# A graph layer's gathers: 71 single rows per half step in place of 40, fetched by two other queues

## Chip, cores and metric

The kernel runs on one core of a Trainium2 chip. The metric is device time in microseconds for one execution; the kernel before takes 15340.11 us in the median of three runs (15320.92 to 15340.7). The profiled execution is a fourth one.

## What is computed

There are 50,000 nodes with 128 features each and 1,650,000 edges, sorted by destination. 50,000 of the edges are self-loops, one for each node. The reference, cut down:

```
Xs  = x[src]
msg = where(edge_type == 0, Xs @ W_data.T + b_data, Xs @ W_control.T + b_control)
agg = segment_sum(msg, dst)
h   = relu(agg + x @ W_self.T + b_self)
out = layernorm(x + h)
```

For each edge a row of 512 bytes is fetched from `x`, and the rows are summed by destination and type. The kernel sums the raw rows first (two sums per node, one for each type) and multiplies the sums by the weights afterwards.

## The kernel before

The program is unrolled over NBLK = 510 steps. Each step but the first and the last takes BE = 3236 edges, in Q = 2 half steps of 1618. The edges of a half step are served in three ways:

- **1536 by gathers**: 12 columns of 128 edges. For each column GpSimd issues one indirect DMA (L477, `gathers`) that fetches 128 rows of `x` into a tile `y`. A tile holds PASS = 6 columns, and there are SLOTS = 10 such tiles, so GpSimd may run up to 60 gathers ahead of TensorE. That is 24 gathers for a whole step.
- **F = 42 fillers**: in the 1536 places some edges are self-loops, whose row need not be gathered because the step's own nodes are loaded in any case (`xT`, L406). `fill` (L316 to L338, VectorE) puts 42 other edges into 42 such places of the half step and notes which self-loops it pushed out. These are added from `xT` later (L345 to L370, L525).
- **S = 40 single rows**: plain DMAs of 512 bytes, each with its address in a register. TURNS = (20, 20) says how many of a half step's rows SP's queue and ScalarE's queue (ACT) issue. For the step, that is 40 copies on each.

`single_rows(b, part)` issues the single rows. A row of byte offsets, `at_x`, is written for the step by VectorE (L435). Each of the LOADS = 2 parts loads its share of the offsets into registers of the queue's engine with one load instruction (TENSOR_LOAD, L446, here 20 registers), and then issues a register move and a DMA for each row (L451). SP and ACT work side by side, each through its own half of `at_x`. When all rows of a step have landed, TensorE uses them in one product for each half step (L502), after the twelve gathered columns (L496).

**Order.** The schedule is written out by hand in the last loop of `straight`, and every engine follows its instructions in that order. Within step b the loop over four passes of six gathers places, among others:

- pass 0: six columns of products, then `layer(b-1)` (TensorE, L531 to L535), `moments(b-1)`, `onehot(b+2)`, and `single_rows(b+2, 0)`;
- pass 1: six columns, the first half's single rows (`rows_fetched` is TensorE's wait for them), `add(b, 0)` (L512), `root(b-1)` (ACT, L551), `counts(b+2)` (L420), `single_rows(b+2, 1)`;
- pass 2: six columns, `store(b-1)` (VectorE, L557 to L559), `fill(b+5)`;
- pass 3: six columns and the second half's single rows, `offsets(b+3)` (L435), `store_rows(b-1)` (SP, L563). The next step begins with `window(b+4)` (SP, L406) and `add(b, 1)`.

So on SP's queue, in each step: the parts of `single_rows(b+2)`, the store of the finished rows of step b-1 (which waits for VectorE's L559), the load of `xT` (with a load of five base registers in every fifth step, L400), and in every tenth step the loads of the edge lists of the next ten steps (L165 to L174) and the two transfers at L301 and L306. On ACT's queue: part 0 of `single_rows(b+2)`, the square root of step b-1, then the other part. The single rows of step b are therefore issued during step b-2, as soon as VectorE has written their offsets in step b-3's last pass. Four sets of `yx`, the tile that the rows land in, rotate (ROW_SLOTS).

The last step takes what is left: 3040 edges, all by gathers (24 of them). With the first step's 24 that makes 510 x 24 = 12,240 gathers. Ahead of the loop, VectorE prepares steps 1 to 4, and the single rows of step 1 are issued there.

Of the kernel before, what the change touches and what calls it, by code (L numbers as in the profile page):

```python
# [36 lines left out]
Q = 2  # L37
PASS = 6
B = 112
C = R * Q  # L40
F = 42
TURNS = (20, 20)
S = sum(TURNS)
LOADS = 2
X = Q * S
R1 = R + 1
C1 = Q * R1
SIZES = [P] * R
SIZE = sum(SIZES)
CE = Q * SIZE  # L50
BE = CE + Q * F + X
NBLK = 2 + (E - CE) // BE
REST = E - CE - (NBLK - 2) * BE
REST_ROWS = [min(n, max(0, REST - q * SIZE - sum(SIZES[:r]))) for q in range(Q) for r, n in enumerate(SIZES)]
# [23 lines left out]
TBL = GROUPS * GB  # L78
# [3 lines left out]
def plain(b):  # L82

    return b == 0 or b >= NBLK - 1
# [6 lines left out]
def straight(ctx, tc, c, x, x_t, src_t, dst_t, etype_t, src_f, dst_f, etype_f, src_x, dst_first, first_p, out):  # L91
# [35 lines left out]
                   allow_small_or_imprecise_dtypes=True)  # L127
    FILL = Q * F + C1
    small = keep_ps.tile([P, 2 * W + F + 2 * FILL + 2], F32, name="small")
    num_ps, rank_no_ps = small[:, :2 * W], small[:, 2 * W:2 * W + F]  # L130
    lists = [small[:, 2 * W + F + i * FILL:][:, :FILL] for i in range(2)]
    sums_at = [small[:Q * F, 2 * W + F + 2 * FILL + i:][:, :1] for i in range(2)]

# [29 lines left out]
    def load_edges(g):  # L163
        t = eds.tile([1, GB * X], I32, name="one_g")
        nc.sync.dma_start(t, src_x[None, g * GB * X:(g + 1) * GB * X])  # L165
        one_g[g] = t
        loads[g] = {}
        for name, a in (("s", src_t), ("d", dst_t), ("t", etype_t)):
            t = eds.tile([P, GB, C1], I32, name=name, bufs=1)
            nc.sync.dma_start(t.rearrange("p b c -> p (b c)"), a[:, g * GC:(g + 1) * GC])  # L170
            loads[g][name] = t
        for name, a in (("sf", src_f), ("df", dst_f), ("tf", etype_f)):
            t = eds.tile([GS, F], I32, name=name, bufs=1)
            nc.sync.dma_start(t, a[g * GS:(g + 1) * GS, :])  # L174
            loads[g][name] = t
# [54 lines left out]
    def check(d, rel, at, name):  # L230
        chk = eds.tile(list(d.shape), F32, name="chk" + name, bufs=1)
        nc.vector.scalar_tensor_tensor(chk, d, float(DST_PAD), rel, op0=ALU.is_lt, op1=ALU.mult)
        axes = AX.XY if len(d.shape) == 3 else AX.X
        nc.vector.tensor_reduce(at[0], chk, axes, ALU.min)
# [74 lines left out]
    def fill(b):  # L309
# [15 lines left out]
        v = fil.tile([P, C1], F32, name="v_new")  # L325
        nc.vector.tensor_reduce(v, new, AX.X, ALU.add)  # L326
        vi = fil.tile([P, C1], I32, name="vi")
# [9 lines left out]
        with nc.allow_low_precision(reason="whole numbers below 256, one of them not 0"):  # L337
            nc.vector.tensor_reduce(by, old.rearrange("p (q r) f -> p q f r", r=R1), AX.X, ALU.add)  # L338
        bys[b] = by
# [76 lines left out]
    def counts(b):  # L416

        cnt = ohp.tile([P, Q, 2 * W], BF16, name="cnt")
        with nc.allow_low_precision(reason="whole numbers up to R1"):
            nc.vector.tensor_reduce(cnt, ohs[b].rearrange("p (q r) w -> p q w r", r=R1), AX.X, ALU.add)  # L420
        cnts[b] = cnt
# [8 lines left out]
    def offsets(b):  # L430

        if not plain(b):
            g, i = divmod(b, GB)
            ats[b] = stp.tile([1, X], I32, name="at_x", bufs=AHEAD + 2)
            nc.vector.tensor_scalar(ats[b], one_g[g][:, i * X:(i + 1) * X], float(ROW), None, op0=ALU.mult)  # L435

    def single_rows(b, part):

        if part == 0:
            ys[b] = stp.tile([S, Q, D], F32, name="yx", bufs=ROW_SLOTS)  # L440
        both = []
        for j, (eng, dma) in enumerate(((SP, nc.sync), (ACT, nc.scalar))):
            n = Q * TURNS[j]
            k0, k1 = part * n // LOADS, (part + 1) * n // LOADS
            at = Q * sum(TURNS[:j])
            _, rows = nc.values_load_multi_w_load_instructions(ats[b][0:1, at + k0:at + k1], engines=[eng], **RANGE)  # L446
            both.append([(dma, fetched[j][b % ROW_SLOTS], *divmod(k0 + k, TURNS[j]), sum(TURNS[:j]), row)
                         for k, row in enumerate(rows)])
        for pair in zip_longest(*both):
            for dma, sem, q, k, at, row in filter(None, pair):  # L450
                copy = dma.dma_start(ys[b][at + k:at + k + 1, q, :].bitcast(U8), x_bytes[:, bass.ds(row, ROW)])  # L451
                copy.then_inc(sem, 16)
                tc.no_tile_sem_insts.add(copy.ins.name)
                tc.add_to_no_dep_group(f"single{b}", copy.ins)

    def rows_fetched(b):

        times = len(range(b % ROW_SLOTS or ROW_SLOTS, b + 1, ROW_SLOTS))
        for j in range(2):
            wait = nc.tensor.wait_ge(fetched[j][b % ROW_SLOTS], 16 * Q * TURNS[j] * times)  # L460
        tc.declare_fence(wait.ins, group=f"single{b}")
# [141 lines left out]
    for b in range(1, RAHEAD):  # L603
        fill(b)
        left_out_columns(b)
        left_out_matrix(b)
        if b < AHEAD:
            onehot(b)
            counts(b)
            for part in range(LOADS):  # L610
                single_rows(b, part)
        if b == 1:
            clear_sums()
    for b in range(NBLK + 1):
# [16 lines left out]
        for q, (step, ks) in enumerate(passes_of(b)):  # L631
# [26 lines left out]
            if q == 3:  # L658
                left_out_matrix(b + RAHEAD)
                offsets(b + AHEAD + 1)  # L660
            if q < LOADS and not plain(b + AHEAD):
                single_rows(b + AHEAD, q)
# [226 lines left out]
def gnn_resnorm(  # L889
# [50 lines left out]
    with ExitStack() as own:  # L940
        straight(own, tc, c, x, x_t, src_t, dst_t, etype_t, src_f, dst_f, etype_f, src_x,
                 dst_first, first_p, out)
# [58 lines left out]
```

## Time and profile before

| | |
|---|---|
| median of three runs | 15340.11 us (15320.92 to 15340.7) |
| profiled execution | 15323.45 us |
| its span, first to last instruction | 15321.7 us |
| granted TensorE clock, mean | 0.535 |
| GpSimd busy (DMA_INDIRECT) | 11565.0 us, 75% |
| VectorE busy | 10904.6 us, 71% |
| TensorE busy, matmul / weight load | 8296.6 us, 54% / 7096.5 us, 46% |
| ScalarE busy | 153.6 us, 1% |
| q0 (GpSimd's gathers) | 802.93 MB, 20.9% of the 16 DMA engines' time |
| q1 (SP) / q10 (ACT) | 112.76 MB, 2.9% / 10.68 MB, 0.3% |

An engine's busy time counts only its working instructions. Register, branch, semaphore and DMA-issuing instructions do not count as busy, so SP does not appear in the table, and ACT's 1% leaves out all its copies. Both are seen only in the timeline of their queues (SPq, ACTq) and in the list of the instructions of one line. In the timeline a row is a merged run of like instructions: its start, its length from the first one's start to the last one's end, and how many there were.

### The profile page before, as it was taken

What the parts mean: (1) busy time and instruction counts of PE and PEld (TensorE: products, weight loads), DVE (VectorE), ACT (ScalarE), POOL (GpSimd) and SP (SyncE); (2) the same over time, 40 slices, a digit from 0 to 9 for tenths busy, and PEclk for the clock granted to TensorE, in tenths of its full rate; (3) what the DMA queues carried; (4) which work ended last, traced back from release to release, by engine and by line L of the source; (5) the groups of instructions that cost most, each with busy time, mean ns of one, the idle gap of its engine ahead of it and who ended that gap; (6) DMA issues with size and microseconds to landing.
All of it is one profiled execution on the core that took longest, in us unless ns stands there. A gap on an engine that the chain in (4) does not pass through costs nothing. (4 is left out here: it accounts for less than half of the span.)

```text
span 15321.7 us, 197234 instructions
## 1 busy us (share of the span) xinstructions
PE 8296.6 (54%) x35844; PEld 7096.5 (46%) x35845; DVE 10904.6 (71%) x13994; ACT 153.6 (1%) x516; POOL 11565.0 (75%) x12250
## 2 busy tenths in 40 slices
PE   3555555555555555555555555555555555555555
PEld 3444444444444444444444444444444444444444
DVE  8777777777777777777777777777777777777775
ACT  0000000000000000000000000000000000000000
POOL 7777777777777777777777777777777777777777
PEclk7555555555555555555555555555555555555555
DMA  2222222222222222222222222222222222222222
GB/s 65 62 61 62 61 62 61 62 62 61 62 61 62 61 62 61 62 61 62 62 60 62 61 62 61 62 62 61 61 62 62 61 62 61 62 61 62 62 61 56
DMA packets 649293, 939.07 MB, mean 61 GB/s; under 512 B 327756, under 2 KB 445487, under 8 KB 648034
## 3 DMA queue, kind: packets, MB, share of 16 engines
q0 software_dynamic: 391680, 802.93, 20.9%
q1 hardware_dynamic: 215276, 112.76, 2.9%
q10 hardware_dynamic: 41078, 10.68, 0.3%
q14 instruction: 968, 7.93, 0.2%
q8 instruction: 291, 4.77, 0.1%
HBM read 895.92 MB, written 29.42 MB: 60 GB/s over the span
## 5 line engine op out<-in xcount | busy, mean ns | idle before, releaser
L477 POOL DMA_INDIRECT y<-in_x,idx x12216 | 11540.9, 945 | 3733.3 <-issue 3552.2
L496 PE MATMUL acc<-oh,y 128*128 128x120 f32 x24480 | 5867.6, 429 | 5768.3 <-PEq L484 5767.8
L496 PEld LDWEIGHTS acc<-oh,y 128*128 128x128 f32 x24480 | 5313.7, 326 | 6190.7 <-PEq L484 6178.3
L420 DVE TENSOR_REDUCE cnt<-oh 128x240 bf16<-128x3120 f32 x510 | 2959.6, 5803 | 0.1
L541 DVE COPY h<-po 112x128 f32<-112x128 f32 x510 | 148.7, 292 | 2499.1 <-PE po L535 2407.5
L412 DVE TENSOR_TENSOR oh<-col,small 128x3120 f32<-128x3120 f32 x510 | 1719.5, 3372 | 0.0
L512 DVE TENSOR_TENSOR sums<-acc,sums 128x180 f32 x1020 | 352.2, 345 | 1393.1 <-PE acc L505 1236.0
L338 DVE TENSOR_REDUCE by<-old 128x84 bf16<-128x1092 f32 x508 | 1078.5, 2123 | 17.6
L502 PE MATMUL acc<-oh,yx 40*128 40x120 f32 x2032 | 777.4, 484 | 0.0
L345 PE MATMUL small<-ones_b,by 128*84 128x1 bf16 x508 | 117.4, 231 | 1191.1 <-DVE by L338 1191.1
L319 DVE TENSOR_TENSOR m<-rk,small 128x1092 f32<-128x1092 f32 x508 | 656.4, 1292 | 17.3
L322 DVE TENSOR_TENSOR new<-m,small 128x1092 f32<-128x1092 f32 x508 | 656.2, 1292 | 17.3
L326 DVE TENSOR_REDUCE v_new<-new 128x26 f32<-128x1092 f32 x508 | 655.8, 1291 | 17.3
L345 PEld LDWEIGHTS <-by 128*84 128x84 bf16 x508 | 74.3, 146 | 1267.3 <-DVE by L338 1267.2
L335 DVE TENSOR_TENSOR old<-m,small 128x1092 f32<-128x1092 f32 x508 | 652.3, 1284 | 0.0
L502 PEld LDWEIGHTS acc<-oh,yx 40*128 40x128 f32 x2032 | 497.5, 304 | 210.0 <-issue 205.3
L535 PE MATMUL po<-wmsgT,sums 128*112 128x128 f32 x2040 | 515.1, 396 | 0.0
L535 PEld LDWEIGHTS po<-wmsgT,sums 128*112 128x112 f32 x2040 | 374.0, 253 | 108.2 <-issue 88.7
L533 PE MATMUL po<-bias,sums 3*112 3x128 f32 x1020 | 350.3, 439 | 0.0
L525 DVE TENSOR_TENSOR sums<-pl,sums 128x336 f32<-128x336 f32 x508 | 257.9, 508 | 85.2 <-DVE sums L512 84.6
L532 PE MATMUL po<-wselfT,xT 128*112 128x128 f32 x1020 | 315.5, 412 | 0.0
L551 ACT ACTIVATE sd<-mv,eps 112x1 f32<-112x1 f32 x510 | 150.4, 295 | 15051.3 <-DVE mv L546 8335.5
(118 smaller groups left out, 4174.2 us busy)
## 6 DMA issues: line engine op xcount, KB each, us to landing
yx<-in_x ACTq DMA_DIRECT2D x20320, 0.5 KB
yx<-in_x SPq DMA_DIRECT2D x20320, 0.5 KB
y<-in_x,idx POOLq DMA_INDIRECT x12216
xT<-in_x_t SPq DMA_DIRECT2D x510, 56.0 KB
out<-o SPq DMA_DIRECT2D x510, 56.0 KB
vf_all<-vd SPq DMA_DIRECT2D x51, 420.0 KB
s<-in_src_t SPq DMA_DIRECT2D x51, 130.0 KB
d<-in_dst_t SPq DMA_DIRECT2D x51, 130.0 KB
```

The costliest lines, as they stand in the source:

```text
L319: nc.vector.tensor_tensor(m, rk_g[g][:, i, :, None].to_broadcast([P, C1, F]), rank_no_ps[:, None, :].to_broadcast([P, C1, F]), op=ALU.is_e ...
L322: nc.vector.tensor_tensor(new.rearrange("p (q r) f -> p q r f", r=R1), m.rearrange("p (q r) f -> p q r f", r=R1), vf.rearrange("p (q f) -> ...
L326: nc.vector.tensor_reduce(v, new, AX.X, ALU.add)
L335: nc.vector.tensor_tensor(old, m, cb[:, :, None].to_broadcast([P, C1, F]), op=ALU.mult)
L338: nc.vector.tensor_reduce(by, old.rearrange("p (q r) f -> p q f r", r=R1), AX.X, ALU.add)
L412: nc.vector.tensor_tensor(oh, col_g[g][:, i, :, None].to_broadcast([P, C1, 2 * W]), num_ps[:, None, :].to_broadcast([P, C1, 2 * W]), op=AL ...
L420: nc.vector.tensor_reduce(cnt, ohs[b].rearrange("p (q r) w -> p q w r", r=R1), AX.X, ALU.add)
L477: copy = nc.gpsimd.indirect_dma_start(out=y[:r, k % PASS, :].bitcast(U8), out_offset=None, in_=x_rows, in_offset=bass.IndirectOffsetOnAxis ...
L496: nc.tensor.matmul(acc[:, :2, :].rearrange("p t w -> p (t w)"), y[:r, k % PASS, :], ohs[b][:r, column(k), :], start=k == of_step[0], stop= ...
L502: nc.tensor.matmul(acc[:, :2, :].rearrange("p t w -> p (t w)"), ys[b][:, q, :], ohs[b][:S, q * R1 + R, :], start=False, stop=True)
L512: nc.vector.tensor_tensor(part, accs.pop((b, q)), part, op=ALU.add)
L535: nc.tensor.matmul(po, a[:, t, :B], c["wmsgT"][:, t * D:(t + 1) * D], start=False, stop=t == 1)
```

## The change

Three constants, the split of a half step's single rows into parts, and the layout of the offsets:

```diff
-F = 42
-TURNS = (20, 20)
+F = 43
+TURNS = (35, 36)
 S = sum(TURNS)
-LOADS = 2
-X = Q * S
+LOADS = 3
+BEGIN = (0, -(-Q * TURNS[0] // 4) * 4)
+X = BEGIN[1] + -(-Q * TURNS[1] // 4) * 4
...
-BE = CE + Q * F + X
+BE = CE + Q * (F + S)
...
+    def part_of(n, part):
+
+        return n if part == LOADS else -(-part * n // (4 * LOADS)) * 4
+
...
-            k0, k1 = part * n // LOADS, (part + 1) * n // LOADS
-            at = Q * sum(TURNS[:j])
+            k0, k1 = part_of(n, part), part_of(n, part + 1)
+            at = BEGIN[j]
```

S becomes 71, and a step takes 3072 + 2 x (43 + 71) = 3300 edges. For a whole step SP issues 70 copies and ACT 72. Each queue's rows come in three parts (passes 0, 1 and 2) of 24, 24 and 22 registers on SP and 24, 24 and 24 on ACT. The parts begin at offsets 0, 24 and 48 of `at_x` for SP and at 72, 96 and 120 for ACT; `at_x` has 144 entries in place of 80. The rest of the diff lays the host's list of offsets out in the same way. There are 2 + (1650000 - 3072) // 3300 = 501 steps, and 228 edges are left for the last one, which are two gathers (128 and 100 rows).

## Prediction

> **What bounds the kernel now.** I read the costliest groups first, then the waits, then the timeline of GpSimd's queue in mid-run.
>
> ```profile
> L477 POOL DMA_INDIRECT y<-in_x,idx x12216 | 11540.9, 945 | 3733.3 <-issue 3552.2
> ...
> L420 DVE TENSOR_REDUCE cnt<-oh 128x240 bf16<-128x3120 f32 x510 | 2959.6, 5803 | 0.1
> ```
>
> GpSimd does little else than issue gathers: 945 ns busy each, and the idle time between them is nearly all "issue", in which it waits for nothing that the profile shows.
>
> ```profile
> 7004.21 0.94 POOL L477 DMA_INDIRECT y<-in_x,idx  x1 [0.30 <-issue]
> 7005.45 0.95 POOL L477 DMA_INDIRECT y<-in_x,idx  x1 [0.30 <-issue]
> 7006.71 0.94 POOL L477 DMA_INDIRECT y<-in_x,idx  x1 [0.30 <-issue]
> ```
>
> So a gather starts every 1.25 us, busy engine or not. The first starts at 3.2 us and the last at 15305.3 (the line's own list): 15302.1 / 12239 = 1.2503 us. 24 of them make a step of 30.0 us. Since 12,240 x 1.25 is the whole span, **the kernel's time is the number of gathers times 1.25 us**, plus 16.4 us after the last one's start. VectorE works 10904.6 / 510 = 21.4 us of those 30, TensorE's matmuls 16.3. They wait.
>
> The two queues that issue the single rows wait too. For SP the waits, the list of the load's and the copies' lines, and its timeline:
>
> ```profile
> SPq L446 <- DVE sums L525: 4574.7, 482, 41.1
> ```
>
> ```profile
> L446 ACTq TENSOR_LOAD <-at_x x1016: 1411/1437/1689, 16.8 to 15202.4; - x170
> L446 SPq TENSOR_LOAD <-at_x x1016: 1197/1378/1676, 26.8 to 15191.8; - x170
> ```
>
> ```profile
> L451 SPq MOVE yx<-in_x x20320: 29/29/37, 28.0 to 15199.5; - x200
> L451 SPq DMA_DIRECT2D yx<-in_x x20320: 224/228/389, 28.1 to 15199.6; - x200
> ```
>
> ```profile
> 7014.69 14.42 SPq L451 DMA_DIRECT2D yx<-in_x  x40
> 7029.38 0.34 SPq L563 DMA_DIRECT2D out<-o  x1
> 7029.90 0.36 SPq L406 DMA_DIRECT2D xT<-in_x_t  x1
> 7030.36 0.36 SPq L306 DMA_DIRECT2D vf_all<-vd  x1
> 7039.36 14.90 SPq L451 DMA_DIRECT2D yx<-in_x  x40
> ```
>
> The reader is to see that a burst of 40 copies takes SP some 14.7 us and that it then idles for 7 to 9 us until the next step's offsets are written. The change fills this room. The question is whether it overfills it.
>
> **The gathers that go.** 501 steps make 500 x 24 + 2 = 12,002 gathers, 238 fewer. At 1.25 us (no stall among those removed) that is 297.5 us. At the end a little comes back: the last step has 2 gathers in place of 24, so the end of the step before it no longer lies beside them. After its last gather follow the landing (2.4 us in the chain of before), 12 products, `find_bad`, two `add`s, and two layers with their moments one after the other. By the rows of the last 20 us of before I count 21.4 us from the last gather's start in place of 16.4, so +5. With GpSimd as the bound: 15321.7 - 297.5 + 5 = **15029 us of span**.
>
> **SP's step, before.** From the timeline between 7005 and 7310 us, ten bursts: 14.42, 14.90, 14.90, 14.47, 14.84, 14.83, 14.85, 14.46, 14.82, 14.85, mean 14.73 us, each with one load of 20 registers inside. Ahead of it lies the first load (1.36 us on the idle queue) with 0.12 us of gaps: 1.48. Other work of the step: store and `xT` 1.15 (7029.11 to 7030.26), a base load of 1.17 every fifth step (0.24), the ten-step group's nine DMAs (0.39). Sum 1.78. In all 1.48 + 14.73 + 1.78 = **17.99 us** of 30.
>
> **SP's step, after:**
> - 30 more copies. In a burst, a load amid it costs 1.58 us (1.46 right behind copies, gaps 0.06, a slower first copy 0.06). So a copy takes (14.73 - 0.23 - 1.58) / 39 = 0.33 us. Added: 9.90. Bounds: 0.322 from the shortest burst, 0.334 from the longest.
> - A third load: 1.58.
> - More registers in a load: 24, 24 and 22 for 20. The trace has no such load. One register takes SP 0.473 us (L943), five take 0.75 where they begin at a multiple of four and 1.30 where they don't (L400: 714/1286/1386), 20 take 1.36. This fits a price of 0.22 us for each group of up to four: (1.36 - 0.473) / 4. I take this, since it alone explains the two prices of L400: one more group in each of three loads is 0.66. Below it, by registers alone, (1.36 - 0.473) / 19 x 10 = 0.47. Above, 3 x 0.25 = 0.74, from 1.46 behind copies.
>
> Sum: 17.99 + 9.90 + 1.58 + 0.66 = **30.1 us**, with the low prices 29.7, with the high ones for every copy and load 30.6. Against GpSimd's 30.0 this is a tie, and it leans to SP.
>
> The page "Runtime: NRT & Kernel Launch" of the Trainium skill (Instruction fetch mechanics) speaks against the change: a register load costs about 200 ns for each register, even in bulk. This trace agrees only for L400's five registers that don't begin at a multiple of four (1.30 us); 20 in 1.38 to 1.44 us are 70 ns each. By the page, SP's 70 registers would cost 14 us and the step would be some 39 us, 19,600 us in all as an estimate.
>
> **ACT's step.** By the same count over its records it works 16.7 us of 30 now. 32 more copies at 0.327 (10.45), a third load with its slower first copy (1.77) and three more groups of registers (0.74) make 29.6. It stays under both, so it is hidden. Without SP's limit it would be next.
>
> **What the span is if SP is the bound.** SP can't hide its lag for long, for the start already uses the reserve. VectorE writes the offsets of step 3 only at 103.3 us, since it fills four steps first. Before, SP then has its rows issued in 16 us and the engines catch up about 5 us per step (their own work is 25 us). After, steps 3 to 499 follow without a pause: 497 steps x 30.1 from 103.5. Behind the last row come its landing and the products that it held back (some 10 us) and the end as above (19), less 1.8 of SP's work that comes later: + 27. So the span is 130 + 497p for a step of p us, and GpSimd's bound of 15029 takes over at p = 29.98. For p = 30.1: 130 + 14965 = **15095 us**. The profiled run's time was 1.75 us over its span: **15097**. That execution was 17 us under the median of the runs shown, within their scatter.
>
> **What costs nothing.** F = 43 lengthens five VectorE operations of a step by 1/42 (1.29 x 4 + 2.12, so 0.17 us) and the offsets by 64 numbers (below 0.1): hidden, as VectorE has 8 us to spare. A longer contraction in L502 (71 rows for 40) is the same instruction. Rows land late only if SP is late, which is counted. The gather's pitch doesn't suffer: among intervals with four SP copies in them it is 1.249 us, as in those with none. ACT's square root comes behind 24 copies in place of 20 (1.6 us later), and VectorE needs it only after 5.8 us of `counts`; without that cover `store` would stall 1.6 us per step, within the 8. The fillers need 43 self-loops in each half step; in the given edges the fewest is 43, so it just suffices and the general path isn't taken.
>
> **Rivals.**
> - **A: SP fits.** The offsets' loads cost by registers, or the copies run at their clear-run pitch of 0.3215 us (the median) when the queues no longer start in step with each other. Then p is under 29.98 and GpSimd keeps the bound: 15031 us. For it: the shortest bursts. Against: one copy in 67 has a gap of 0.33 us more, which grows with the number of copies.
> - **C: the copies slow down (slower).** Both queues now issue without a break. In the trace the second to sixth copies of a burst, where ACT starts beside SP, have a mean pitch of 0.331 to 0.346. Were all at 0.346, p = 30.1 + 70 x 0.016 = 31.2 and the time 130 + 497 x 31.2 = 15640. It decides from 0.338 (p = 30.66, 15370 us). Against: whole bursts stay at 0.334 or less.
> - **D: 24 registers don't fit one load**, so the change gives more loads than three. Three more (0.47 + 0.06 each) give p = 31.7: 15885 us. For it: no load in the trace has more than 20.
>
> **How the numbers follow.** B, the forecast (SP bound by a little, p from 29.98 to 30.66): 0.57; A 0.33; C 0.07; D 0.03. Differences under 0.2% are about what a measurement of this kernel can't tell from none; that band, 15309 to 15371, is the top of B (p over 30.53), 0.04. So faster 0.86, same 0.04, slower 0.10. The range goes from just under A's time, 15015, to p = 30.42, which is 15250: it leaves out C, D, and the top of B.
>
> **What would show it.** Gathers: 12,002 at 0.944 us. If B holds, SP's queue has no wait for offsets left, bursts of 70 stand 30.1 us apart, and GpSimd waits for TensorE's products (its tiles come free late), while TensorE waits for the single rows. If A, GpSimd's idle stays all "issue" and SP still idles a little. In both, loads of 24 registers take 1.58 to 1.7 us and copies 0.32 to 0.334. A load over 1.9 us or a pitch over 0.338 makes the prediction wrong.

## The result and the profile after

The changed kernel takes **15829.25 us** (median of four runs, 15826.12 to 15832.71), the kernel before 15340.1: a ratio of 1.0321 (95% interval 1.0305 to 1.0337). It is 3.2% slower, where 1.6% faster was forecast (15097). The profiled run took 15827.65 us, its span 15826.0.

GpSimd did lose its 238 gathers, and a gather takes as long as before. But now it stands still between them. Of the profile after, the costliest groups and the waits (engine, line, whom it waited for: us in total, times, longest):

```profile
L482 POOL DMA_INDIRECT y<-in_x,idx x12000 | 11339.4, 945 | 4422.8 <-issue 3422.7
```

```profile
PE acc L507 <- PEq L465: 3218.0, 392, 21.3
...
POOL y L482 <- PE acc L501: 792.8, 187, 11.1
```

GpSimd waits 793 us for a tile that TensorE hasn't used yet (L501). TensorE in turn stands at L507, the product of the single rows, behind L465: its wait until all rows of the step have landed. The list of that line's instructions shows how long one such wait lasts (minimum / median / maximum in ns). The first row is from the kernel before, where the line is L460, the second from after:

```profile
L460 PEldq EVENT_SEMAPHORE  x508: 51/51/51, 106.9 to 15263.1; - x170
```

```profile
L465 PEldq EVENT_SEMAPHORE  x499: 51/10226/23226, 108.1 to 15790.9; - x167
```

Before, the rows were always there. After, this wait lasts 10 us in the median step, and TensorE itself is idle for 3218 / 499 = 6.4 us of each step because of it. So the single rows set the pace. Who is late with them? SP's waits and its timeline:

```profile
SPq L175 <- DMA out<-o: 534.4, 49, 12.9
SPq L451 <- DVE mv L551: 40.9, 41, 1.8
```

```profile
7026.04 0.35 SPq L568 DMA_DIRECT2D out<-o  x1
7026.63 1.58 SPq L407 DMA_DIRECT2D xT<-in_x_t  x1
...
7030.63 0.34 SPq L175 DMA_DIRECT2D df<-in_dst_f  x1
7041.17 0.28 SPq L175 DMA_DIRECT2D tf<-in_edge_type_f  x1
7043.34 26.71 SPq L456 DMA_DIRECT2D yx<-in_x  x70
7070.31 0.35 SPq L568 DMA_DIRECT2D out<-o  x1
7070.89 0.36 SPq L407 DMA_DIRECT2D xT<-in_x_t  x1
7073.03 26.81 SPq L456 DMA_DIRECT2D yx<-in_x  x70
```

SP hardly waits for offsets any more (L451: the largest row is 41 us; L446 had 4575 us before). It works 30.5 us of each step, by the sum of its records and the short gaps between them. Yet a step takes 31.6 us, and the rest is one wait that wasn't there before: in every tenth step the last of the edge lists (`tf`, L175) stands 10 us. Its instruction uses the same completion semaphore as the store of rows (`out`) issued eight DMAs earlier at 7026.04, and waits until that has landed. The rows land as late; the chain that ended last holds such landings (start, length):

```profile
7025.50 15.02 DMA yx<-in_x
7069.82 11.56 DMA yx<-in_x
7221.04 8.27 DMA yx<-in_x
```

A copy of 512 bytes takes up to 15 us from its issue to its landing. From the trace's semaphore events I took, for each step between 1,000 and 14,000 us, the time from the last issue to the last landing of SP's rows: before 2.8 to 4.0 us, after 3.1 to 15.1. It grows by about 1.5 us from step to step for seven steps, from 4 us to 14 or 15, and falls back over the next three: SP stands at L175 for 10 us, and ACT then stands 15 us before a load of offsets. **The copies pile up behind the queues.**

The same events show where. A load of `xT` tells of its landing in sixteen events, and the profile counts 16 DMA engines. Medians from the start of its issue, for the loads with all sixteen events in the trace:

| | 15 of the 16 have come | all 16 |
|---|---|---|
| before | 1.90 us | 1.97 us |
| after | 1.96 us | 10.1 us |
| ACT's rows left out (an experiment below) | 1.89 us | 1.94 us |

Fifteen shares of `xT` land as early as before, and one lands as late as the rows. The store of `out` shows the same (1.65 and 10.1 us after the change), which is why it keeps L175 waiting. So the backlog lies in one place out of sixteen, and whatever has a share there waits with the copies.

### The profile page after: what moved, and what is told of

Its sections match the earlier page's. It is cut to its first block, busy times and chain, and to the rows that moved or that the text cites. A ratio compares the mean times of both kernels' runs of the same rounds, so it can differ in the third digit from the quotient of the medians.

```text
span 15826.0 us, 256554 instructions
## 1 busy us (share of the span) xinstructions
PE 6610.8 (42%) x35177; PEld 6147.3 (39%) x35178; DVE 10848.4 (69%) x13768; ACT 150.8 (1%) x507; POOL 11342.8 (72%) x12012
## 4 chain that ended last, share of the span: by engine, by line
SPq 35%; DVE 23%; DMA 15%; issue 14%; PE 8%; ACTq 4%; DVEq 0%; ACT 0%; PEldq 0%; PEld 0%
SPq L456 27%; DMA yx<-in_x 14%; SPq L451 7%; DVE cnt L421 5%; PE acc L501 4%; ACTq L456 4%; DVE by L339 3%; DVE m L320 2%; DVE new L323 2%; DVE v_new L327 2%; DVE old L336 2%; PE po L540 1%; PE acc L507 1%; DMA out<-o 1%; PE po L538 1%
## 5 line engine op out<-in xcount | busy, mean ns | idle before, releaser
L482 POOL DMA_INDIRECT y<-in_x,idx x12000 | 11339.4, 945 | 4422.8 <-issue 3422.7
L501 PE MATMUL acc<-oh,y 128*128 128x120 f32 x24004 | 4836.7, 384 | 0.1
L501 PEld LDWEIGHTS acc<-oh,y 128*128 128x128 f32 x24004 | 4598.7, 293 | 0.2 <-PE po L593 0.2
L507 PE MATMUL acc<-oh,yx 71*128 71x120 f32 x1996 | 560.2, 373 | 3218.4 <-PEq L465 3218.0
L507 PEld LDWEIGHTS acc<-oh,yx 71*128 71x128 f32 x1996 | 405.7, 253 | 3316.6 <-PEq L465 3316.0
L339 DVE TENSOR_REDUCE by<-old 128x86 bf16<-128x1118 f32 x499 | 1080.4, 2165 | 17.3
L320 DVE TENSOR_TENSOR m<-rk,small 128x1118 f32<-128x1118 f32 x499 | 658.6, 1320 | 17.0
L323 DVE TENSOR_TENSOR new<-m,small 128x1118 f32<-128x1118 f32 x499 | 658.5, 1320 | 17.1
L327 DVE TENSOR_REDUCE v_new<-new 128x26 f32<-128x1118 f32 x499 | 657.4, 1317 | 17.0
L336 DVE TENSOR_TENSOR old<-m,small 128x1118 f32<-128x1118 f32 x499 | 654.2, 1311 | 0.0
```

Of the source, the lines that this page charges most:

```text
L320: nc.vector.tensor_tensor(m, rk_g[g][:, i, :, None].to_broadcast([P, C1, F]), rank_no_ps[:, None, :].to_broadcast([P, C1, F]), op=ALU.is_e ...
L323: nc.vector.tensor_tensor(new.rearrange("p (q r) f -> p q r f", r=R1), m.rearrange("p (q r) f -> p q r f", r=R1), vf.rearrange("p (q f) -> ...
L482: copy = nc.gpsimd.indirect_dma_start(out=y[:r, k % PASS, :].bitcast(U8), out_offset=None, in_=x_rows, in_offset=bass.IndirectOffsetOnAxis ...
L501: nc.tensor.matmul(acc[:, :2, :].rearrange("p t w -> p (t w)"), y[:r, k % PASS, :], ohs[b][:r, column(k), :], start=k == of_step[0], stop= ...
L507: nc.tensor.matmul(acc[:, :2, :].rearrange("p t w -> p (t w)"), ys[b][:, q, :], ohs[b][:S, q * R1 + R, :], start=False, stop=True)
```

## The theories

- *Landing*: the copies of both queues pass one place that takes some 0.22 us for each. SP and ACT hand over 142 in the 30.5 us that SP works for a step, the place needs about 31.6, and the backlog grows until something waits for a landing.
- *Issue* (the forecast, with more in it): SP's instructions are the bound, 30.5 us, and the wait at L175 is an accident of the order, worth 1.1 us per step.

A step's length is given below as the mean distance of SP's stores, over whole tens of steps between 1,000 and 14,000 us; it is 31.57 us for the changed kernel and 29.99 for the one before. The runs with registers loaded once, without ACT's rows and with 1 KB are one execution each; the kernel before, run beside them, took 15,322 to 15,356 us.

## Experiments

**Registers loaded once.** Takes 5.3 us of SP's work out of every step. All rows fetched are those of 24 offsets, hence the wrong ones.

```diff
-            _, rows = nc.values_load_multi_w_load_instructions(ats[b][0:1, at + k0:at + k1], engines=[eng], **RANGE)
+            if j not in held:
+                _, held[j] = nc.values_load_multi_w_load_instructions(ats[b][0:1, at:at + 24], engines=[eng], **RANGE)
+            rows = [held[j][k % 24] for k in range(k0, k1)]
```

> Registers are loaded once per queue (24 of them) and every later copy takes its address from them, so the rows fetched are the wrong ones; numbers and sizes of copies stay. The changed kernel has a step of 31.6 us, of which SP works 30.5 us (5.3 of them register loads) and waits 1.1. Theory 'issue' (SP's instructions are the bound): SP's step falls to 25.2 us, GpSimd is the bound again, about 15,030 us. Theory 'landing' (the copies of both queues pass one place that needs some 0.22 us for each, 31.6 to 32 us for 142): the step stays at 31.6 to 32, 15,830 to 16,040 us, with rows landing more than 10 us after their issue in every step.

Measured: 15858.55 us, a step of 31.67 us. SP's saved work bought nothing. In its place come waits and slower issues, as the timeline of this run shows: a burst of 70 is shorter (23 us), then L175 waits 18 us, and the DMAs ahead of it take 0.7 to 2.6 us to issue, where they took 0.3 to 0.5:

```profile
7033.77 2.56 SPq L175 DMA_DIRECT2D sf<-in_src_f  x1
7036.38 1.34 SPq L175 DMA_DIRECT2D df<-in_dst_f  x1
7055.92 0.28 SPq L175 DMA_DIRECT2D tf<-in_edge_type_f  x1
7056.31 22.96 SPq L460 DMA_DIRECT2D yx<-in_x  x70
```

The rows land 11 to 28 us after their issue. *Issue* has fallen as the account of the last 1.1 us.

**The same with 160 copies** (`TURNS = (40, 40)`), for the price of a copy.

> As the run with registers loaded once (wrong rows), but 80 rows per half step, so 160 copies per step and 498 steps of 24 gathers. Issue: SP works 80 x 0.333 + 2 = 28.6 us per step, GpSimd is the bound, about 14,950 us. Landing: the step grows with the copies, 35 to 35.8 us, 17,400 to 17,800 us.

Measured: 17387.27 us, a step of 34.96 us. SP's issues would fit well into 30 us. The time follows the number of copies: 34.96 / 160 = 0.218 us, 31.67 / 142 = 0.223. The difference of the two runs gave me some 0.184 us for a copy and 5.4 us for a step beside it; the expectations of the later runs go by these two numbers.

**The wait at L175 taken away.** The lists are asked for after the second part of the rows, so that the semaphore's earlier user has had time to land. The result is the same.

```diff
-        if i == 0 and g + 1 < GROUPS:
-            load_edges(g + 1)
...
             if q < LOADS and not plain(b + AHEAD):
                 single_rows(b + AHEAD, q)
+            if q == 1 and i == 0 and g + 1 < GROUPS:
+                load_edges(g + 1)
```

> The edge lists of the next ten steps are asked for after the second part of the single rows, not at the start of the step; then the last of them no longer reuses the completion semaphore of a store issued just before. The same result. Issue: the wait of 11 us in every tenth step goes, the step falls from 31.6 to SP's 30.5, about 15,290 us. Landing: the pause only let the copies that had piled up drain; without it the step is no shorter than 31.6, 15,830 to 16,040 us.

Measured: 15856.43 us (ratio to before 1.0341, 1.031 to 1.0371), a step of 31.66 us. The timeline shows the lists issued without a stop, and a burst of 70 that now lasts 29.00 us where it took 26.7:

```profile
7006.28 29.00 SPq L456 DMA_DIRECT2D yx<-in_x  x70
...
7059.16 0.34 SPq L175 DMA_DIRECT2D df<-in_dst_f  x1
7059.55 0.44 SPq L175 DMA_DIRECT2D tf<-in_edge_type_f  x1
```

The time that stood in the wait has gone into the copies themselves, whose mean distance rose from 0.332 to 0.347 us. The landing lag is 10 to 17 us and no longer falls back to 4. So the wait was a symptom.

**ACT's rows left out.** The sums lack ACT's 36 rows per half step; TensorE contracts over SP's 35 only.

```diff
-        for j, (eng, dma) in enumerate(((SP, nc.sync), (ACT, nc.scalar))):
+        for j, (eng, dma) in enumerate(((SP, nc.sync),)):
...
-        for j in range(2):
+        for j in range(1):
             wait = nc.tensor.wait_ge(fetched[j][b % ROW_SLOTS], 16 * Q * TURNS[j] * times)
```

> ACT's 72 copies and its loads are left out (their rows are missing from the sums). SP does all of its own. Landing: 70 copies per step don't pile up, the store lands early, SP's wait goes and its own work of 30.5 us is the bound: about 15,290 us, with SP never idle. Issue: if the wait of 1.1 us is SP's own affair, the step stays at 31.6, 15,830 us.

Measured: 15223.1 us, a step of 30.36 us, in which SP never idles (no gap of over 0.4 us between its records from 1,000 to 14,000 us): this is SP's own limit. The rows land 0.9 to 1.6 us after their issue. SP issues the same 70 copies at the same pace as in the changed kernel, so what made them land late is the other queue's copies.

**Twice the bytes.** Each copy brings 1 KB, the row and the one behind it, into a wider tile; a single row of the very last node is replaced by its neighbour.

```diff
-                copy = dma.dma_start(ys[b][at + k:at + k + 1, q, :].bitcast(U8), x_bytes[:, bass.ds(row, ROW)])
+                copy = dma.dma_start(ys[b][at + k:at + k + 1, q, :].bitcast(U8), x_bytes[:, bass.ds(row, 2 * ROW)])
```

> 71 copies of 1 KB (row and neighbour) per half step, on a chip on which the kernel before takes its usual time. Price for a copy as such: 15,830 to 15,860 us. Price for bytes: 28,800 us. If the second half KB costs its own packet time only, some 0.02 us per copy: 34.4 us per step, 17,250 us.

Measured: 15897.83 us, a step of 31.72 us. The second half KB costs (31.72 - 31.57) / 142 = 0.001 us a copy, no more than the runs at 512 bytes differ by (31.57 to 31.67). The price is for the copy, not for its bytes.

**Fewer rows, a correct kernel: 69 and 66 per half step.** Only `TURNS` differs from the changed kernel, (34, 35) and (33, 33); the 43 fillers, the three loads and their layout stay.

> 69 rows per half step, on such a chip. Landing: 5.4 + 138 x 0.184 = 30.8 us per step, 130 + 497 x 30.8 = 15,435 us; GpSimd alone would need 15,045, SP 30.0 us per step.

Measured: 15195.39 us (ratio 0.9917, 0.9888 to 0.9946), a step of 30.32 us. That is over GpSimd's 30.0 and over SP's own work of 29.4 (the sum of its records), so the limit of the landings still sets the time: the rows land 6 to 15 us after their issue, and SP waits 463 us at L175. But my two numbers for it were off: 5.4 + 138 x 0.184 gave 30.8. A price for each copy with nothing beside it fits better: 30.32 / 138 = 0.220.

> 66 rows per half step, on a chip on which the kernel before takes 15,320 to 15,360 us. Landing: 5.4 + 132 x 0.184 = 29.7 us per step, under GpSimd's 30.0, SP 29.0: GpSimd is the bound, about 15,075 us. If the third load or the 43 fillers cost the time: above 15,340.

Measured: **15082.73 us** (two runs; ratio to before 0.9844, 0.9815 to 0.9873), as forecast. 132 x 0.22 = 29.0 us per step, and GpSimd is the bound again. In this run its waits are "issue" as in the kernel before, and the wait for the rows is nothing in the median step:

```profile
POOL y L482 <- issue: 3530.3, 11564, 0.3
POOL y L482 <- PE acc L501: 56.4, 174, 3.6
```

```profile
L465 PEldq EVENT_SEMAPHORE  x500: 51/51/18728, 107.7 to 15032.7; - x167
```

This version beats both kernels. It has the third load and the 43 fillers, so neither of them cost the time.

**Runs that can't be compared.** Ten runs fell on chips where the kernel before itself takes 19,240 to 19,300 us in place of 15,320. There SP's and ACT's instructions stand still for 0.7 us at a time in mid-burst; why is open. Nothing above rests on these runs.

Two of the edits were tried only there: each copy in 2 pieces, or (with `a=16`) in 16, to put its bytes on more DMA engines.

```diff
-copy = dma.dma_start(ys[b][at + k:at + k + 1, q, :].bitcast(U8), x_bytes[:, bass.ds(row, ROW)])
+copy = dma.dma_start(ys[b][at + k:at + k + 1, q, :].bitcast(U8).rearrange("p (a c) -> p a c", a=2),
+                     x_bytes[:, bass.ds(row, ROW)].rearrange("p (a c) -> p a c", a=2))
```

> Each single row is asked for as two pieces of 256 bytes in one DMA (the same result). The runs with 142 and 160 copies give the place that the copies pass as 5.4 us per step plus 0.184 us per copy. If the price is for bytes and the two pieces go to two DMA engines, a copy costs about half, the landing limit is gone, and SP's own 30.4 us is the bound: about 15,230 us. If the price is for a copy (its descriptors on the first engine), nothing is gained: 15,830 us or more. If pieces are not spread at all, each piece has its price and the step is up to 5.4 + 284 x 0.184 = 57.7 us, 28,800 us.

> 71 rows as two pieces of 256 bytes in one DMA, once more on a usual chip. Price for bytes and the pieces on two engines: no landing limit, SP's 30.4 us is the bound, about 15,230 us. Price for a copy on the first engine: 15,830 us or more. Pieces not spread and each with its price: up to 28,800 us.

> As before with sixteen pieces of 32 bytes (the same result). Price for bytes: about 15,230 us if issuing stays as cheap. Price for a copy on the first engine: 15,830 us or more. A price for each piece on each of sixteen engines also gives 15,830, as each engine has one piece of each copy.

Measured: 25,255 and 25,263 us with 2 pieces, 25,324 with 16, one execution each. The pieces lie side by side, and the profile shows one element of 512 bytes again, so these were the changed kernel unaltered, and whether spreading a row would help is open.

66 rows, `TURNS = (33, 33)`, four times:

> 66 single rows per half step (33 by each queue), all else as in the changed kernel: 502 steps, 12,040 gathers, 132 copies per step. Landing: 5.4 + 132 x 0.184 = 29.7 us, under GpSimd's 30.0; SP's work 30.37 - 4 x 0.333 = 29.0. So GpSimd is the bound: 12,040 x 1.25 + 25 = 15,075 us, 1.7% under the kernel before. A theory in which the third register load or the 43 fillers cost the time would leave it above 15,340.

> The kernel with 66 rows per half step once more, on a chip on which the kernel before takes its usual 15,320 to 15,360 us (the chip of the last four runs took 19,300 for it, as SP's and ACT's instructions stood still there for 0.7 us at a time). Landing: 5.4 + 132 x 0.184 = 29.7 us per step, under GpSimd's 30.0, SP 29.0: GpSimd is the bound, about 15,075 us. If the third load or the 43 fillers cost the time: above 15,340.

> 66 rows per half step, on a chip on which the kernel before takes 15,320 to 15,360 us. Landing: 5.4 + 132 x 0.184 = 29.7 us per step, under GpSimd's 30.0, SP 29.0: GpSimd is the bound, about 15,075 us. If the third load or the 43 fillers cost the time: above 15,340.

> 66 rows per half step, on a chip on which the kernel before takes 15,320 to 15,360 us. Landing: 5.4 + 132 x 0.184 = 29.7 us per step, under GpSimd's 30.0, SP 29.0: GpSimd is the bound, about 15,075 us. If the third load or the 43 fillers cost the time: above 15,340.

Measured: 24,366, 24,312, 24,383 and 24,315 us, 1.26 to 1.27 times the kernel before on the same chips; the run told above replaces them.

69 rows, `TURNS = (34, 35)`:

> 69 single rows per half step (34 and 35): 501 steps, 138 copies per step. Landing: 5.4 + 138 x 0.184 = 30.8 us per step, 130 + 497 x 30.8 = 15,435 us, though GpSimd alone would need 15,045 and SP 29.7 us per step. If SP's issuing is the bound: 15,050 us.

Measured: 24,849 us, 1.2885 times the kernel before there [1.2863, 1.2906].

Copies of 1 KB, twice, with the edit shown above:

> Each single-row copy brings 1 KB, the row and the one behind it, into a wider tile; the second row isn't used (and a single row of the very last node would be replaced by its neighbour). Copies, issues and waits stay, bytes double. In the changed kernel the copies' place needs 5.4 us per step plus 0.184 us per copy. Price for a copy as such: nothing changes, 15,830 to 15,860 us. Price for bytes: 5.4 + 142 x 0.368 = 57.7 us per step, 28,800 us. In between, if the second half KB costs only its own packet time (some 0.02 us, from the 1040-byte packets' 46 ns against 27 for 512): 31.6 + 2.8 = 34.4 us, 17,250 us.

> 71 copies of 1 KB (row and neighbour) per half step, on a chip as above. Price for a copy as such: 15,830 to 15,860 us. Price for bytes: 28,800 us. If the second half KB costs its own packet time only, some 0.02 us per copy: 34.4 us per step, 17,250 us.

Measured: 25,207 and 25,193 us, as much as the runs at 512 bytes (25,255 to 25,324) to within 0.6%.

## Why the prediction was wrong

- *The gathers that go*: right. 12,002 of them at 945 ns, and 66 rows gave the time that this step of the sum gives.
- *SP's step, after*, 30.1 us: nearly right, and of use. SP alone works 30.36 us, and 130 + 497 x 30.36 = 15,219 against 15,223 measured. The error of 0.26 is mostly in the loads. SP's three loads of 24, 24 and 22 registers take 1.58, 1.69 and 1.89 us in the mean, the shortest list the longest. With 66 rows SP loads 24, 20 and 22, in 1.58, 1.46 and 1.89 us: the last two of the 22 cost 0.43 us, as much as two groups. So the price by groups of four registers fits full groups, but not a rest of two, and a load of 24 would have been cheaper. Two small slips in the sums change nothing: the shortest and longest burst give bounds of 0.323 and 0.336 us for a copy, not 0.322 and 0.334, and 497 x 30.1 is 14,960, not 14,965.
- *"Rows land late only if SP is late, which is counted"*: **this is the step that failed.** I priced the copies where they are issued and took their landing to be free. The landings have a limit of their own, some 0.22 us for each copy of either queue, and 142 copies need 31.6 us. The limit accounts for 15,829 - 15,223 = 606 us; SP's own length, against GpSimd's bound, for 15,223 - 15,031 = 192.
- *What would show it*: nearly all the signs named for SP as the bound came: no long wait for offsets, GpSimd waiting for TensorE, TensorE for the rows, loads of 24 and copies within their limits. They can't tell rows that are issued late from rows that land late. Only the distance of the bursts, 31.6 us in place of 30.1, and the landings can.
- *What the span is*: the formula 130 + 497p held: 15,820 for 31.57 (15,826 measured), 15,199 for 30.32 (15,192).
- *Rivals C and D* had the sign and not the mechanism: the mean distance of SP's copies is 0.332 us in both kernels, and there are three loads. *ACT's step*, 29.6, was 30.0 by its records.
- *The Trainium skill's 200 ns per register* (page "Runtime: NRT & Kernel Launch", section "Instruction fetch mechanics"): 70 registers cost SP 5.2 us, not 14. It agrees with the last two of the 22, 0.43 us for both.

The trace of before held the sign. In a burst of 14.7 us the two queues together issue 80 copies, one in 0.184 us, which is faster than 0.22; and the last row landed 3.3 us after its issue in the median, where it is 1.2 with SP alone. The pause after each burst let it drain. I counted 7 to 9 us of that pause as free room for SP, and never asked what the landings had free. At 0.22 us each, 80 copies take 17.6 us of a step of 30 and leave 12.4; the 62 added copies need 13.6.

Why should both queues share a limit? The Trainium skill, page "DMA: Bandwidth & Descriptors", section "Why a DMA increments its semaphore by 16 and not by 1", says that a DMA whose shape in the instruction is [1, 1] goes to a single DMA engine, and on the queues of SP and ACT to the lowest-numbered. The profile gives the copies this shape, with one element of 512 bytes. That would put all 142 copies on one engine of 16. The trace agrees: each copy raises its semaphore in two events (10,042 for 5,080 copies on one of them in the trace before), one at issue and one at landing, and of the sixteen events of `xT` one alone is late. It doesn't name the engine that moved a packet, and no run here moved the copies to another. So that it is one place for both queues, one of the sixteen that a wide transfer uses, with a price per copy, is shown; that this place is the engine of the lowest number is the page's account.

What makes up the 0.22 us stays open. The packets of ACT's copies took 1.3% of 16 engines' time, 0.09 us a copy. The wait lies ahead of them: the packet of 512 bytes began 7.2 us after the start of its copy's issue in the median, where it was 0.95 us before.

## What to carry to other kernels

Two queues that issue many small DMAs side by side may have a common limit behind them. Before filling a pause, look at the last landing after a burst: if it is later with both queues than with one, the pause is not free. A wide transfer with one late share, like `xT` here, shows the same backlog. Take the price per copy over the whole period, both queues together (here 0.22 us), beside each queue's price of issuing (0.33 us).

## What was not expected of the hardware

- Single-row copies of 512 bytes and of 1 KB pass at the same rate, 0.218 to 0.223 us each over six runs with 138 to 160 copies per step.
- The limit doesn't show as a slow queue at first. The issues keep their pace of 0.332 us while the landing lag grows from 3 to 15 us. In the runs with longer lags the mean was 0.347 us (10 to 17 us, the wait at L175 gone) and 0.39 (11 to 28 us, the loads gone).
- One of the sixteen shares of a wide transfer can be 8 us later than the other fifteen, because of small copies ahead of it.
- A register load costs by groups: 24 registers 1.58 to 1.69 us, 22 registers 1.89 us on SP.
